# Two result chains in one-bank tiles, taken out block by block, and a half sum made from another sum

## The chip, the cores and the metric

The kernel runs on one core of a Trainium2 chip. The metric is the device time in microseconds (us) of one execution. TensorE (PE in the profile) multiplies, VectorE (DVE) adds and subtracts, ScalarE (ACT) applies functions and casts, GpSimd (POOL) issues the gathers and scatters, and SyncE (SP) issues most of the loads. Each engine takes its instructions strictly in the order in which they are written in this kernel, and waits in place where an operand is not ready.

## The reference

For 4096 tokens of 1024 features, after a layer norm:

```python
q, k, v = xn @ Wq.T + bq, xn @ Wk.T + bk, xn @ Wv.T + bv
kv_sum  = cumsum((elu(k) + 1) * v, axis=1)
s = ((elu(q) + 1) * kv_sum * 64**-0.5) @ Wo.T + bo
h = gelu(buf @ w1.T + b1) @ w2.T + b2        # buf: tokens chosen by a router
g = silu(scattered(h, router weights))
out = x + s * g
```

The router keeps at most 256 tokens for each of 8 experts, so the products with `w1`, `w2`, `Wq` and `Wo` are needed for at most 2048 tokens: `g` is zero for the rest, and their `out` is `x`.

## The kernel before

**Stages.** A first stage (to 444.66 us) makes the norm, the keys, the values and their running sum, and the router's lists. The second, which the change is about, takes the 2048 chosen tokens in two passes (`p` = 0, 1) of 1024. A pass makes the feed-forward part in four slices (`hidden`, then `ffn_out`), then the queries (`queries`) and the output projection (`result`). Each of these ten steps of a pass is a 1024x1024x1024 product, done as seven half-size products by a scheme of Strassen's kind: a weight or token quarter, or a sum of quarters (`t`, and sums written into the quarters' own places), against another. So there are 2 x 10 x 7 = 140 half-size products. The text numbers them 1 to 140 in order of time: 57 to 63 are the queries of pass 0 and 64 to 70 its output projection; 127 to 133 and 134 to 140 are the same of pass 1. "The crossing" is the stretch from the queries to the output projection, around products 62 to 66 and again around 132 to 136.

**A product.** It is 48 matmuls of 128x128 on 128x512 (L1023). Each float is split into a high part (a cast on ACT, L799) and the rest (a subtraction on DVE, L802, called "low" here), and three of the four part products are made, hence 2 halves `u` x 4 blocks `m` x 2 x 3 = 48. Half `u` of an operand is cast and split while the product before runs: `cast0`, `low0`, `cast1`, `low1` in the list below. The usual order is all four blocks of half 0, then all four of half 1; only the very last product goes block by block.

**Results.** A product's result is a tile `ps` of four PSUM banks, one for each block of 512. Products that are added up without anything in between form a chain in one tile (`chains`); PSUM has room for two such tiles (pool `fps`), and the built program uses them by turns: every product writes the four banks that the one before did not write. DVE takes a result out in one instruction (L951: `plus`, or `more` and `last` in `features`).

**The order of the work** is written out by hand. `multiply(n)` issues product n; then the hooks of step n follow, phase by phase: `load`, `pre`, `cast0`, `evac`, `low0`, `add`, `cast1`, `low1`, `post`, `raw`. `on(n, phase, f)` puts a piece of work there. So what stands in phase `evac` of step n takes out product n-1 while product n runs, and on ACT and DVE everything waits for what stands earlier.

**Around the crossing.** `features` takes the last results of the queries out with `last`: product 61 at step 62, 62 at step 63, and 63 at step 64. For each, `act` of `queries` runs a Relu and an Exp for each of four blocks on ACT (L1257, L1258), and `then` at phase `post` of the same step makes four DVE operations L1263 and two L1268. The quarter `(0, 1)` comes from product 63. `left_tokens` then makes three half sums on DVE from the four finished quarters: `t` = h01 + h11 (L951) at `post` of step 64, behind `then`, and h01 = h00 - h01 and h00 = t - h00 (L948 twice) at `pre` of step 65. h00, so changed (S2 here), is the left operand of product 66, and h01, so changed (S3), that of product 68. `result` takes product 64 out twice at step 65 (`e1`: three DVE instructions, the last of which writes `y`), product 65 at step 66 (`c11`), and so on; `done` scatters a quarter to DRAM with four indirect DMAs from POOL that add to what lies there (L1328), after the whole quarter is ready.

**The end.** `last` in `result` takes products 138 and 139 out in one piece each, and the last product, 140, in four blocks.

**The start.** The second stage's two PSUM tiles lie where the first stage had its pools `trp` (banks 0 to 3) and `mmp` (banks 4 to 7). The first stage's last value products are in `mmp`, and DVE takes them out in L401.

## Time and profile before

Three runs gave 2052.49, 2051.97 and 2054.68 us, a median of 2052.49. The execution with a profile took 2053.1 us, of which 2051.3 us are the span from its first to its last instruction.

| engine | busy us | share of the span |
|---|---|---|
| PE | 1968.8 | 96% |
| DVE | 1513.0 | 74% |
| ACT | 756.7 | 37% |
| POOL | 398.3 | 19% |

The profile's timeline lists instructions as "start, duration, engine, line, operation, what it writes and reads, count", with the idle time of the engine before it, and what ended that, in square brackets; equal neighbours are merged. The view by stretches of time gives, for each stretch, each engine's busy time and number of instructions, the share of full speed at which TensorE's clock was granted (PEclk), and the DMA engines' busy share and rate. A product that waits for nothing takes 10.88 us (48 matmuls, 0.227 us from start to start).

### The profile page before, as it was taken

To read this page: it belongs to the slowest core of one execution; us is meant where nothing else is said; L and a number is where in the kernel's file an instruction comes from. 1 tells how busy PE (TensorE), PEld (TensorE's weight loads), DVE (VectorE), ACT (ScalarE), POOL (GpSimd) and SP (SyncE) were. 2 spreads that over 40 slices of the span, in tenths; PEclk is the share of its full clock that TensorE was granted. 3 is DMA by queue.
4 is the path that set the end of the run, shared out by engine and by line. 5 is a ranking of instruction groups with operands and counts; after the bars stand their busy time and mean duration, and the time that the engine had idled before them with its cause. 6 is when DMAs were issued, how large, how long until landed. Compare 5 with 4: busy or idle time off the path is not lost.

```text
span 2051.3 us, 22262 instructions
## 1 busy us (share of the span) xinstructions
PE 1968.8 (96%) x8840; PEld 1624.9 (79%) x8840; DVE 1513.0 (74%) x1378; ACT 756.7 (37%) x874; POOL 398.3 (19%) x359
## 2 busy tenths in 40 slices
PE   7999999999999999999999799999999999999875
PEld 6877878888887887888888578888888888888664
DVE  7868876679867867875877786775774775786784
ACT  2323332225433524433433453342432432433451
POOL 1001104654002402713040027300000003040013
PEclk9999999999999999999999989999999999999988
DMA  8867848657249349347156049427326327336314
GB/s 308 241 195 239 268 124 189 194 153 299 80 166 362 108 164 343 121 153 282 46 184 254 23 110 307 168 75 249 127 87 249 116 100 257 116 124 235 124 21 63
DMA packets 113842, 360.31 MB, mean 176 GB/s; under 512 B 12768, under 2 KB 37344, under 8 KB 95584
## 3 DMA queue, kind: packets, MB, share of 16 engines
q1 hardware_dynamic: 77504, 299.98, 42.2%
q0 software_dynamic: 17792, 42.55, 7.8%
q10 hardware_dynamic: 18432, 16.26, 3.5%
q8 instruction: 72, 1.18, 0.2%
q14 instruction: 42, 0.34, 0.1%
HBM read 292.66 MB, written 73.42 MB: 178 GB/s over the span
## 4 chain that ended last, share of the span: by engine, by line
PE 78%; DVE 11%; ACT 3%; DMA 3%; issue 3%; POOL 0%; ACTq 0%; SPq 0%; DVEq 0%; POOLq 0%
PE ps L1023 62%; PE pk L160 3%; PE pk L161 3%; PE pk L162 3%; PE pv L162 2%; PE pv L160 2%; PE pv L161 2%; DMA b<-xtd 1%; DVE hid L951 1%; DVE a L802 1%; DVE hid L1263 1%; DVE b L802 1%; DVE raw L948 1%; DMA xtd<-b 1%; PE pl L326 1%
## 5 line engine op out<-in xcount | busy, mean ns | idle before, releaser
L1023 PE MATMUL ps<-b,a 128*128 128x512 f32 x6720 | 1541.1, 392 | 44.2 <-DVE y L951 20.7
L1023 PEld LDWEIGHTS ps<-b,a 128*128 128x128 f32 x6720 | 1269.0, 189 | 315.9 <-ACT b L799 21.5
L799 ACT CAST a<-raw 128x1024 fp32r<-128x1024 f32 x140 | 147.2, 1052 | 434.6 <-PE ps L1023 376.1
L802 DVE TENSOR_TENSOR a<-raw,a 128x1024 fp32r<-128x1024 f32 x140 | 170.6, 1221 | 171.2 <-ACT a L799 171.2
L648 POOL DMA_INDIRECT gk<-kvs,eighth x128 | 156.4, 1222 | 657.8 <-DVE kv L240 620.0
L799 ACT CAST a<-hid 128x1024 fp32r<-128x1024 f32 x120 | 126.0, 1050 | 358.0 <-PE ps L1023 250.4
L802 DVE TENSOR_TENSOR a<-hid,a 128x1024 fp32r<-128x1024 f32 x120 | 146.5, 1221 | 63.8 <-ACT a L799 63.6
L802 DVE TENSOR_TENSOR b<-raw,b 128x1024 fp32r<-128x1024 f32 x140 | 170.7, 1220 | 1.9 <-ACT b L799 1.9
L951 DVE TENSOR_TENSOR hid<-ps,hid 128x2048 f32<-128x2048 f32 x54 | 123.5, 2286 | 54.4 <-PE ps L1023 54.4
L948 DVE TENSOR_TENSOR raw<-raw,raw 128x2048 f32<-128x2048 f32 x70 | 160.3, 2289 | 1.0
L799 ACT CAST b<-raw 128x1024 fp32r<-128x1024 f32 x140 | 146.6, 1047 | 2.1 <-DMA xtd<-b 2.1
L951 DVE TENSOR_TENSOR work<-ps,work 128x2048 f32<-128x2048 f32 x40 | 91.5, 2288 | 48.8 <-PE ps L1023 48.8
L160 PE MATMUL pk<-xt,ws_w 128*128 128x512 f32 (+1 forms) x264 | 102.4, 388 | 1.5 <-ACT xt L166 1.5
L161 PE MATMUL pk<-xt,ws_w 128*128 128x512 f32 (+1 forms) x264 | 102.0, 386 | 1.3 <-DVE xt L167 1.3
L162 PE MATMUL pv<-xt,ws_w 128*128 128x512 f32 (+1 forms) x264 | 101.4, 384 | 1.3 <-DVE ws_w L167 1.2
L162 PE MATMUL pk<-xt,ws_w 128*128 128x512 f32 (+1 forms) x264 | 101.8, 386 | 0.0
L160 PE MATMUL pv<-xt,ws_w 128*128 128x512 f32 (+1 forms) x264 | 101.6, 385 | 0.0
L161 PE MATMUL pv<-xt,ws_w 128*128 128x512 f32 (+1 forms) x264 | 101.2, 383 | 0.0
L166 ACT CAST ws_w<-wr_w 128x1024 fp32r<-128x1024 f32 x64 | 66.1, 1049 | 70.0 <-issue 30.8
L167 DVE TENSOR_TENSOR ws_w<-wr_w,ws_w 128x1024 fp32r<-128x1024 f32 x64 | 77.8, 1215 | 14.7 <-ACT ws_w L166 14.7
L680 POOL DMA_DIRECT2D xtd<-o x28 | 24.2, 888 | 283.3 <-DVE o L167 276.3
L362 ACT ACTIVATE kb<-pk,bs 128x512 f32<-128x512 f32 (+1 forms) x40 | 25.8, 645 | 140.8 <-PE pk L162 106.5
(185 smaller groups left out, 1656.4 us busy)
## 6 DMA issues: line engine op xcount, KB each, us to landing
b<-xtd SPq DMA_DIRECT2D x126, 1024.0 KB, 5.5
raw<-in_w SPq DMA_DIRECT2D x64, 1024.0 KB, 5.2
wr_w<-in_wk SPq DMA_DIRECT2D x32, 512.0 KB, 4.6
wr_w<-in_wv SPq DMA_DIRECT2D x32, 512.0 KB, 4.6
xtd<-b SPq DMA_DIRECT2D x14, 1024.0 KB, 7.7
xtd<-o POOLq DMA_DIRECT2D x28, 512.0 KB, 9.1
kvs<-kr ACTq DMA_DIRECT2D x32, 256.0 KB, 4.9
raw<-in_wq SPq DMA_DIRECT2D x8, 1024.0 KB, 5.1
```

Of the source, the lines that this page charges most:

```text
L160: nc.tensor.matmul(ps, ws[:, 0, k], mv[:, 0, k, c0:c1], start=k == 0, stop=False)
L161: nc.tensor.matmul(ps, ws[:, 0, k], mv[:, 1, k, c0:c1], start=False, stop=False)
L162: nc.tensor.matmul(ps, ws[:, 1, k], mv[:, 0, k, c0:c1], start=False, stop=k == DC - 1)
L166: nc.scalar.copy(dst[0], src)
L167: nc.vector.tensor_tensor(dst[1], src, dst[0].bitcast(F32), ALU.subtract)
L362: nc.scalar.activation(kb, ps, AF.Identity, bias=bcol)
L648: nc.gpsimd.indirect_dma_start(out=dst, out_offset=None, in_=src, in_offset=bass.IndirectOffsetOnAxis(ap=idx, axis=0),)
L799: nc.scalar.copy(self.parts[0], src)
L802: nc.vector.tensor_tensor(self.parts[1], self.src, self.parts[0].bitcast(F32), ALU.subtract)
L948: nc.vector.tensor_tensor(dst, a, b, ALU.subtract)
L951: nc.vector.tensor_tensor(dst, a, b, ALU.add)
L1023: nc.tensor.matmul(ps[:, m], a(h, k, m), b(l, k), start=s["first"] and u == 0 and k == 0 and i == 0, stop=u == 1 and k == 1 and i == 2, sk ...
```

## The change

Three things are changed.

1. Each of the two places of four banks gets a pool of its own. `banks` gives a new chain the place that the preceding product does not write, either as one tile of four banks or, where the chain is marked `apart`, as four tiles of one bank. Marked are the chain of products 61 and 63 (and 131 and 133), and the chain of products 136, 138 and 140.
2. Marked chains are taken out a block at a time. In the queries, product 61 goes out in four instructions in place of one, and product 63 is multiplied block by block and taken out, each block with its own Relu and Exp, at four spots: `add`, `low1` and `post` of step 63 and `pre` of step 64. At the end, products 136, 138 and 139 are taken out by blocks, and blocks of 138 and 139 are scattered one by one.
3. In all ten output steps, S2 is made first, at `pre` of the old step, and S3 one step later, as h11 - S2, which is the same as h00 - h01.

In the built program the first product's place is banks 4 to 7, and products alternate from there; before, it was banks 0 to 3. No other engine than PE, DVE and ACT has another order.

```diff
-    fps = ctx.enter_context(tc.tile_pool(name="fps", bufs=2, space=PSUM, reuse_waits="tile"))
+    places = [[None, None, ctx.enter_context(ExitStack())] for _ in range(2)]
+    last_place = [0]
+    def banks(apart):
+        i = last_place[0] = 1 - last_place[0]
+        place = places[i]
+        if place[0] != apart:
+            place[2].close()
+            place[:2] = apart, place[2].enter_context(
+                tc.tile_pool(
+                    name=name("fps"), bufs=1, space=PSUM, side=("left", "right")[i],
+                    reuse_waits="tile",
+                )
+            )
+        if apart:
+            return i, [
+                place[1].tile([P, BT], F32, tag=f"ps{m}", name=name("ps")) for m in range(4)
+            ]
+        return i, place[1].tile([P, 4, BT], F32, tag="ps", name=name("ps"))
...
-            s["ps"][0] = fps.tile([P, 4, BT], F32, tag="ps", bufs=2, name=name("ps"))
+            s["place"][0], s["ps"][0] = banks(s["apart"])
+        last_place[0] = s["place"][0]
...
-        if n == len(plan):
+        if s["apart"] and s["last"]:
             order_of.sort(key=lambda um: um[1])
...
-        on(n0 + 2, "pre", lambda: sub(h[0, 1], h[0, 0], h[0, 1]))
         on(n0 + 2, "pre", lambda: sub(h[0, 0], h["t"], h[0, 0]))
+        on(n0 + 3, "pre", lambda: sub(h[0, 1], h[1, 1], h[0, 0]))
...
-            plus(h[key], ps[k][0], h[base])
+            for m, x in blocks(ps[k][0]):
+                plus(h[key][:, m], x, h[base][:, m])
...
-        on(n0 + 8, "evac", lambda: last(7, (0, 1), (0, 1)))
+        if not then:
+            on(n0 + 8, "evac", lambda: last(7, (0, 1), (0, 1)))
+            return h
+        def block(m):
+            key = (0, 1)
+            plus(h[key][:, m], ps[7][0][m], h[key][:, m])
+            act(h[key], h[key], *key, blocks=(m,))
+        for d, phase, m in ((7, "add", 0), (7, "low1", 1), (7, "post", 2), (8, "pre", 3)):
+            on(n0 + d, phase, lambda m=m: block(m))
...
-            rows_of = range(4) if n0 + k == len(plan) else [slice(0, 4)]
-            for v in rows_of:
-                plus(c[base][:, v], ps[k][0][:, v], c[base][:, v])
+            parts = blocks(ps[k][0])
+            if p == NP - 1 and k == 6:
+                parts = [(m, ps[k][0][:, m]) for m in range(4)]
+            for v, x in parts:
+                plus(c[base][:, v], x, c[base][:, v])
                 nc.vector.tensor_tensor(c[base][:, v], c[base][:, v], y[key][:, v], ALU.mult)
-            done(key, lambda m: c[base][:, m])
+                done(key, lambda m: c[base][:, m], range(4) if len(parts) == 1 else (v,))
```

More of the change, by code (lines that the diff above doesn't have):

```diff
@@ L911, in tile_first_tokens, with blocks @@
     )
-    fps = ctx.enter_context(tc.tile_pool(name="fps", bufs=2, space=PSUM, reuse_waits="tile"))
+    places = [[None, None, ctx.enter_context(ExitStack())] for _ in range(2)]
[16 more added lines that the diff above has]
+        return i, place[1].tile([P, 4, BT], F32, tag="ps", name=name("ps"))
+    def blocks(ps):
+        if isinstance(ps, list):
+            return [(m, x) for m, x in enumerate(ps)]
+        return [(slice(0, 4), ps)]
     bq1, nbq = (cp.tile([P, DC], F32, name=n) for n in ("bq1", "nbq"))
@@ L1023, in multiply @@
                     nc.tensor.matmul(
-                        ps[:, m],
+                        ps[m] if s["apart"] else ps[:, m],
                         a(h, k, m),
@@ L1037, in tile_first_tokens, with chains @@
     COLS = (1, 2, 6, 5, 7, 3, 4)
-    def chains(n0, order, groups):
-        where = {i: [None] for g in groups for i in g[:1]}
+    def chains(n0, order, groups, apart=False):
         for g in groups:
+            where, place = [None], [None]
             for i in g:
                 k = order.index(i)
-                plan_at(n0 + 1 + k).update(first=i == g[0], ps=where[g[0]])
+                plan_at(n0 + 1 + k).update(
+                    first=i == g[0], last=i == g[-1], ps=where, place=place,
+                    apart=apart and order[-1] in g,
+                )
     def left_weights(n0, src, order):
@@ L1133, in features @@
         if order == ROWS:
-            chains(n0, order, ((1, 2), (6, 7, 4), (5, 3)))
+            chains(n0, order, ((1, 2), (6, 7, 4), (5, 3)), then is not None)
         else:
@@ L1186, in hidden, with outputs @@
         )
-    def outputs(n0, h, src, ahead=0):
+    def outputs(n0, h, src, ahead=0, final=False):
         left_tokens(n0, h)
         right_weights(n0, src, ahead)
-        chains(n0, COLS, ((1,), (2,), (6, 7, 4), (5, 3)))
+        chains(n0, COLS, ((1,), (2,), (6, 7, 4), (5, 3)), final)
         return {k: plan_at(n0 + k)["ps"] for k in range(1, 8)}
@@ L1245, in turn, with act @@
                     )
-        def act(dst, src, i, j):
-            if dst is src:
-                r = [small("ex") for _ in range(2)]
-                r = [r[m // 2][:, m % 2 * BT : (m % 2 + 1) * BT] for m in range(4)]
-            else:
-                r = [dst[:, m] for m in range(4)]
-            kvt["r", i, j] = r
-            for m in range(4):
+        def act(dst, src, i, j, blocks=range(4)):
+            if 0 in blocks:
+                if dst is src:
+                    r = [small("ex") for _ in range(2)]
+                    r = [r[m // 2][:, m % 2 * BT : (m % 2 + 1) * BT] for m in range(4)]
+                else:
+                    r = [dst[:, m] for m in range(4)]
+                kvt["r", i, j] = r
+            r = kvt["r", i, j]
+            for m in blocks:
                 e = 4 * i + m
@@ L1300, in result @@
     def result(n0, h, y, p):
-        ps = outputs(n0, h, wo[0], 1)
+        ps = outputs(n0, h, wo[0], 1, final=p == NP - 1)
         c = {}
@@ L1320, in e1, with done @@
             plus(c[0], ps[1][0], over_blocks(c["b"][:, :BT]))
-        def done(key, parts):
+        def done(key, parts, rows_of=range(4)):
             i, j = key
-            for m in range(4):
+            for m in rows_of:
                 src = parts(m)
@@ L1350, in more @@
             c[key] = h["t" if key == (0, 1) else (0, 1)]
+            if isinstance(ps[k][0], list):
+                for m, x in blocks(ps[k][0]):
+                    plus(c[key][:, m], x, c[1][m // 2][:, m % 2])
+                return
             for half in range(2):
```

## The prediction, made before the changed kernel ran

> **What bounds the kernel now.** I read the page first: PE is busy for 96% of the span, and the chain of work that ended last lies on it but for two kinds of places.

> ```profile
> PE 78%; DVE 11%; ACT 3%; DMA 3%; issue 3%; POOL 0%; ACTq 0%; SPq 0%; DVEq 0%; POOLq 0%
> ```

> The 11% of DVE are in the crossings. PE's own timeline shows it for pass 0: products 62 and 63 run through, and from there every start waits, up to 10.48 us ahead of product 66.

> ```profile
> 1118.50 22.25 PE L1023 MATMUL ps<-b,a 128*128 128x512 f32 x97 [0.96 <-DMA b<-xtd]
> 1141.67 5.74 PE L1023 MATMUL ps<-b,a 128*128 128x512 f32 x24 [0.93 <-DVE b L802]
> 1147.99 5.51 PE L1023 MATMUL ps<-b,a 128*128 128x512 f32 x23 [0.57 <-DVE b L802]
> 1157.53 0.76 PE L1023 MATMUL ps<-b,a 128*128 128x512 f32 x1 [4.03 <-DVE hid L951]
> 1159.71 12.41 PE L1023 MATMUL ps<-b,a 128*128 128x512 f32 x47 [1.41 <-DVE b L802]
> 1182.59 0.76 PE L1023 MATMUL ps<-b,a 128*128 128x512 f32 x1 [10.48 <-DVE y L951]
> 1184.77 720.72 PE L1023 MATMUL ps<-b,a 128*128 128x512 f32 x3167 [1.41 <-DVE b L802]
> ```

> From the start of 62 (1118.50) to that of 67 (1198.07) are 79.57 us for five products of 10.88, so 25.2 us are lost; in pass 1 (1906.61 to 1986.26) 25.3. Some of it is clock. The view by stretches, here product 33, which follows a wait of 2.54 us, and product 66:

> ```profile
> 800.11:812.73 12.62, 12.62 (x49) 10.22 (x49) 9.17 (x11) 4.91 (x7) 2.54 (x3) 0.86 1.02 408
> ```

> ```profile
> 1182.59:1198.07 15.48, 14.07 (x48) 11.01 (x49) 13.66 (x12) 12.80 (x19) 7.22 (x4) 0.76 0.37 50
> ```

> PEclk is the number after POOL's: granted 0.86 and 0.76. Product 33 took 1.74 us too long without a wait inside.

> DVE's timeline then says what the 10.48 us wait for: takings-out of 61, 62 and 63, and `t`, S3 and S2 one behind the other.

> ```profile
> 1122.36 2.28 DVE L951 TENSOR_TENSOR hid<-ps,hid 128x2048 f32<-128x2048 f32 x1
> ...
> 1137.07 2.28 DVE L951 TENSOR_TENSOR hid<-ps,hid 128x2048 f32<-128x2048 f32 x1
> ...
> 1155.10 2.28 DVE L951 TENSOR_TENSOR hid<-ps,hid 128x2048 f32<-128x2048 f32 x1
> ...
> 1171.04 2.29 DVE L951 TENSOR_TENSOR ht<-hid 128x2048 f32<-128x2048 f32 x1
> 1173.37 2.29 DVE L948 TENSOR_TENSOR hid<-hid 128x2048 f32<-128x2048 f32 x1
> 1175.69 2.29 DVE L948 TENSOR_TENSOR hid<-ht,hid 128x2048 f32<-128x2048 f32 x1
> ```

> Between these DVE waits for ACT (3.95 us twice, 5.10 once): the eight Relu and Exp of a quarter (5.13 us in a row) stand ahead of the casts.

> **The change, part by part.**

> *Places.* Products took the two places by turns before and do so after; only the sides are swapped. By itself this is worth nothing: pools are re-opened for products 61, 65, 131, 135 and 136, which in the built order wait for the same results as before. The exception is the start. Product 1 began at 444.66 without a wait, in banks 0 to 3. It now goes to banks 4 to 7, which DVE empties last in:

> ```profile
> 447.11 0.44 DVE L401 SCALAR_TENSOR_TENSOR kb<-pv,bs,kb 128x256 f32<-128x256 f32 x1
> ```

> It ends at 447.55; PE follows DVE by about 0.15 (63 is out at 1155.10 + 2.28 = 1157.38, and 65 starts at 1157.53), so product 1 starts at 447.7: **+3.0 us**. Nothing hides it: the casts, loads and takings-out of the second stage are timed by its products, and shift along. Does the clock drop after it? [...] 2.54 us before product 33 cost 1.74, while 0.96 before 62 cost 0.1 (10.98 us). I take the row: **+1.7**; ends 0 and 3.4 [...]. Start: +4.7, from 3.0 to 6.4.

> *S2 ahead of S3 in the ten output steps.* In the ordinary ones PE does not wait, and S3 is needed two products later. Its 2.3 us of DVE come back ahead of a taking-out that is then due at the old time. One gain: product 10 waited 0.45 us (with its tail 0.6) for ACT, whose copy of a result stood behind the cast of S2; that goes: **-0.6**. In the crossings it is in the sum below.

> *The crossing, pass 0* (before -> after), adding durations in each queue's order:
> - Taking 61 out: starts at 1122.36 as before, but block 0 is done after 0.69 instead of 2.28, so ACT's Relu and Exp start 1.6 earlier, the cast behind them too, and the low that DVE waits for: 1130.88 -> 1129.3. Taking 62 out: 1137.07 -> 1135.5. (Four blocks cost DVE 0.24 more, start to start, hidden by this wait.)
> - Product 63, block by block, needs its second half 1.4 us after its start (1129.48) instead of 5.4: cast by 1129.3, low by 1130.5, in time. Its load is issued at 1124.23 as its place comes free; with the median 5.5 us it lands at 1129.7, needed at 1130.8. With the 7 us of product 62's it stalls 0.5, which the next wait swallows: taken as 0.
> - Low for 64: done at 1140.0, so its wait goes. Blocks 0 and 1 of 63 go out at 1139.9 and 1140.5. But block 0's Relu and Exp (1.29) stand on ACT ahead of 64's second casts: that low 1146.71 -> 1146.4. `then` of 62 ends at 1152.6; block 2, the 2.2 us difference L948, block 3: block 3 done at 1156.1, where 63 as a whole was done at 1157.4.
> - ACT: block 3's Relu and Exp, then both casts for 65: to 1159.4 (these casts stood ahead of the Exp before). So 65's second matmul: 1159.71 -> 1160.9, **later**. DVE goes on without the old wait of 3.95: `then` of 63 starts 1165.88 -> 1163.0; `t` 1171.04 -> 1168.2; S2 1175.69 -> 1170.5, as S3 is gone. `e1`, `y` and the lows follow at once: `y` done 1177.3, 66's second matmul 1184.77 -> 1179.6: -5.2.
> - PE idles about 3.5 us instead of 10.5 ahead of 66, and is at half speed for an estimated 3.7 us after it instead of 5.4: 2.65 lost -> 1.85. Product 67: 1198.07 -> 1192.1. S3 is now in front of 67's lows, done at 1191.2, still ahead of 1192.1.
> So **-6.0**; ends -4.5 [...] and -7. Pass 1 has the same rows 788 us later: **-6.0**. Reading a bank while PE writes its neighbour is shown nowhere before; the nearest row is the end's block, 0.69 us, which I take; a fifth more would be 0.1 a block.

> *The end.* Before, POOL issues eight DMAs from here to there, 1.86 us each:

> ```profile
> 2023.99 1.56 POOL L1328 DMA_INDIRECT out<-ht,half  x1 [2.60 <-DVE ht L1359]
> ...
> 2038.19 1.56 POOL L1328 DMA_INDIRECT out<-y,half  x1 [0.30 <-issue]
> ```

> Now 138's four go from 2008.1 (before 2013.68), done by 2015.4. 139 is out at 2019.1; its block 0 is added and multiplied by 2020.5, so its first DMA is at 2020.8: 3.2 earlier. Product 140's blocks 0 and 1 are ready when POOL is, 2 and 3 at 2028.7 and 2031.4; eight times 1.86 put the last issue at 2033.9, 4.3 earlier. But the DMA engines are 0.94 to 1.04 busy from 2030 to 2042, about 2.1 us a DMA, and the last of their packets ends at 2043.8, 17.9 after the first of these eight: so the end moves with the first: **-3.6**; ends -2 and -4.5. Costs of the extra DVE instructions: DVE waited 1.8 and 6.3 there.

> *Sum*: +4.7 - 0.6 - 12.0 - 3.6 = -11.5. The span 2051.3 becomes 2039.8 and the profiled execution's 2053.1 becomes 2041.6; the median lies 0.6 below that: **2041.0**.

> **The rivals.** (1) As above, 0.6: 2041. (2) The crossing gives half, 0.22: with the Exp of blocks 0 and 3 put ahead of casts, ACT becomes what DVE waits for, as 65's later start shows. That leaves 3 us each: 4.7 - 0.6 - 6 - 3.6 = -5.5, **2047**. Against it: in the walk DVE waits there for under 2 us. (3) No clock drop at the start, and shorter ones in the crossings, 0.13: 1.7 at the start, 2 x 0.85 in the crossings and 0.6 at the end make 4.0 more, **2037**. (4) Slower, 0.05: the clock. The idle ahead of 65 grows from 4.0 to 6.6 us; should TensorE then stay at half speed through 65 and 66, 65 ends at 1160.9 + 21.3 = 1182.2, 66 follows at once and ends at 1204, 6 us later than before: 4.7 - 0.6 + 12 - 3.6 = +12.5, **2065**. It decides once half speed outlasts 65; before, it lasted under 4 us after 65's second matmul.

> **Chances and range.** A measurement of this kernel tells 0.2% (4 us) from no change. (1), (3) and most of (2) are faster: 0.92; 0.03 the same, 0.05 slower. The better ends together (3.0 at the start, -7 twice, -4.5) give 2036.4, and (2) 2047; half a microsecond is added on each side, which leaves out (4) and the tails of (2) and (3).

> **What would show it.** Product 1 starting 3 us after the last value product; lows of 65 later and S2 5 us earlier against 62's start; the wait ahead of 66 at 3 to 5 us; 62 to 67 in 73.6 us; the first `ht` DMA 2 us after 139's end. Wrong if product 1 starts at once, if 62 to 67 takes over 77 us, or if the last bytes land no earlier after 140.

## The result and the profile after

Four runs of the changed kernel gave a median of 2040.62 us (2038.86 to 2042.59), four of the kernel before on the same chip 2053.59 (2051.97 to 2054.71): a ratio of **0.9938 [0.9921, 0.9955]**. The execution with a profile took 2040.5 us with a span of 2038.6, 12.7 less than before; the prediction's sum was -11.5.

The chain of work that ended last has 5 points more of PE and 3 fewer of DVE:

```profile
PE 83%; DVE 8%; ACT 3%; issue 2%; DMA 2%; POOL 1%; ACTq 0%; DVEq 0%; SPq 0%; POOLq 0%
```

PE's timeline, at the start and in both crossings:

```profile
447.50 196.08 PE L1051 MATMUL ps<-b,a 128*128 128x512 f32 x864 [2.68 <-DVE kb L401]
...
1119.93 28.03 PE L1051 MATMUL ps<-b,a 128*128 128x512 f32 x121 [1.17 <-ACT a L799]
1148.89 5.52 PE L1051 MATMUL ps<-b,a 128*128 128x512 f32 x23 [0.94 <-DVE b L802]
1160.63 0.79 PE L1051 MATMUL ps<-b,a 128*128 128x512 f32 x1 [6.22 <-ACT b L799]
1162.08 12.95 PE L1051 MATMUL ps<-b,a 128*128 128x512 f32 x47 [0.66 <-DVE b L802]
1178.61 0.47 PE L1051 MATMUL ps<-b,a 128*128 128x512 f32 x1 [3.58 <-DVE y L978]
1180.78 721.00 PE L1051 MATMUL ps<-b,a 128*128 128x512 f32 x3167 [1.70 <-DVE b L802]
...
1961.62 0.77 PE L1051 MATMUL ps<-b,a 128*128 128x512 f32 x1 [4.22 <-DVE y L978]
1963.80 26.50 PE L1051 MATMUL ps<-b,a 128*128 128x512 f32 x106 [1.41 <-DVE b L802]
```

Product 1 now waits for L401. The wait ahead of 66 is 3.58 us in place of 10.48, and that ahead of 65 is 6.22 in place of 4.03. 62 starts at 1119.93 and 67 at 1194.39: 74.46 us for 79.57 before; in pass 1, from 1902.76 to 1976.76, 74.00 for 79.65. The view by stretches, for product 66 from its first matmul to 67's, shows that the clock is still lost there (PEclk is 0.78; it was 0.76):

```profile
1178.61:1194.40 15.79, 14.09 (x49) 11.14 (x50) 15.58 (x13) 12.80 (x19) 5.54 (x4) 0.78 0.26 35
```

DVE's timeline of the crossing of pass 0 shows the takings-out in pieces, and where DVE itself still waits for ACT:

```profile
1123.58 2.48 DVE L978 TENSOR_TENSOR hid<-ps,hid 128x512 f32<-128x512 f32 x4
...
1141.16 1.28 DVE L978 TENSOR_TENSOR hid<-ps,hid 128x512 f32<-128x512 f32 x2
1146.48 1.23 DVE L802 TENSOR_TENSOR a<-hid,a 128x1024 fp32r<-128x1024 f32 x1 [4.04 <-ACT a L799]
...
1156.60 0.68 DVE L978 TENSOR_TENSOR hid<-ps,hid 128x512 f32<-128x512 f32 x1
1159.67 1.23 DVE L802 TENSOR_TENSOR a<-hid,a 128x1024 fp32r<-128x1024 f32 x1 [2.38 <-ACT a L799]
...
1169.38 2.29 DVE L978 TENSOR_TENSOR ht<-hid 128x2048 f32<-128x2048 f32 x1
1171.71 2.29 DVE L975 TENSOR_TENSOR hid<-ht,hid 128x2048 f32<-128x2048 f32 x1
...
1176.18 2.28 DVE L978 TENSOR_TENSOR y<-ps,bo 128x2048 f32<-128x2048 f32 x1
```

`t` and S2 follow one another without S3, and S2 is done at 1174.00. At the end, POOL's timeline has the first of the last eight DMAs at 2011.29, before 2023.99:

```profile
2011.29 1.56 POOL L1374 DMA_INDIRECT out<-ht,half  x1 [4.61 <-DVE ht L1411]
...
2025.50 1.56 POOL L1374 DMA_INDIRECT out<-y,half  x1 [0.30 <-issue]
```

From 137's start to the last packet of these DMAs it takes 54.01 us (1976.76 to 2030.77), before 57.56 (1986.26 to 2043.81).

| term, us of the span | predicted | measured |
|---|---|---|
| wait ahead of product 1 | +3.0 | +2.84 (444.66 to 447.50) |
| clock at product 1 | +1.7 | 0 (product 1 takes 10.96, before 10.91) |
| wait at product 10 | -0.6 | -0.54 (start of 1 to start of 18: 185.58 to 185.04) |
| crossing, pass 0 | -6.0 | -5.11 |
| crossing, pass 1 | -6.0 | -5.65 |
| the end, from 137 to the last packet | -3.6 | -3.54 |
| clock at product 19 | none | -1.28 (12.62 to 11.34) |
| the rest | 0 | +0.6 (0.34 of it behind the last packet) |
| sum | -11.5 | -12.7 |

### The profile page after: what moved, and what is told of

It is laid out like the page before. It is cut to its first block, busy times and chain, and to the rows that moved or that the text cites. A ratio compares the mean times of both kernels' runs of the same rounds, so it can differ in the third digit from the quotient of the medians.

```text
span 2038.6 us, 22297 instructions
## 1 busy us (share of the span) xinstructions
PE 1967.2 (96%) x8840; PEld 1623.9 (80%) x8840; DVE 1514.1 (74%) x1404; ACT 757.8 (37%) x874; POOL 396.7 (19%) x359
## 4 chain that ended last, share of the span: by engine, by line
PE 83%; DVE 8%; ACT 3%; issue 2%; DMA 2%; POOL 1%; ACTq 0%; DVEq 0%; SPq 0%; POOLq 0%
PE ps L1051 66%; PE pk L160 3%; PE pk L161 3%; PE pk L162 3%; PE pv L162 2%; PE pv L160 2%; PE pv L161 2%; DVE hid L1309 1%; PE pl L326 1%; DVE a L802 1%; DVE raw L975 1%; DVE hid L978 1%; DMA xtd<-o 1%; ACT ex L1303 1%; DMA b<-xtd 1%
## 5 line engine op out<-in xcount | busy, mean ns | idle before, releaser
L1051 PE MATMUL ps<-b,a 128*128 128x512 f32 x6720 | 1539.2, 391 | 36.4 <-ACT b L799 12.7
L802 DVE TENSOR_TENSOR a<-raw,a 128x1024 fp32r<-128x1024 f32 x140 | 170.6, 1221 | 169.6 <-ACT a L799 169.6
L802 DVE TENSOR_TENSOR a<-hid,a 128x1024 fp32r<-128x1024 f32 x120 | 146.4, 1220 | 61.8 <-ACT a L799 61.7
L802 DVE TENSOR_TENSOR b<-raw,b 128x1024 fp32r<-128x1024 f32 x140 | 170.5, 1218 | 1.8 <-ACT b L799 1.8
L978 DVE TENSOR_TENSOR hid<-ps,hid 128x2048 f32<-128x2048 f32 (+1 forms) x69 | 125.0, 1821 | 54.9 <-PE ps L1051 54.9
L166 ACT CAST ws_w<-wr_w 128x1024 fp32r<-128x1024 f32 x64 | 66.1, 1049 | 70.3 <-issue 30.9
L680 POOL DMA_DIRECT2D xtd<-o x28 | 24.2, 888 | 285.5 <-DVE o L167 278.7
```

Source lines behind the costliest of these rows:

```text
L166: nc.scalar.copy(dst[0], src)
L802: nc.vector.tensor_tensor(self.parts[1], self.src, self.parts[0].bitcast(F32), ALU.subtract)
L978: nc.vector.tensor_tensor(dst, a, b, ALU.add)
L1051: nc.tensor.matmul(ps[m] if s["apart"] else ps[:, m], a(h, k, m), b(l, k), start=s["first"] and u == 0 and k == 0 and i == 0, stop=u == 1 ...
```

## The experiments

Theory: the three parts act as the prediction has them, apart from each other; what is left in the crossing is ACT's queue ahead of 65 and the clock after the waits. Rivals: one part makes all of the gain; the order of ACT doesn't matter; what is lost after a wait isn't the clock.

The yardsticks are stretches of the trace. "62 to 67" is the time from the start of 62 to the start of 67, half speed included. "66's second matmul" is its start counted from 62's start, which is free of what the clock does behind it. In two profiles of the kernel before, it comes at 66.1 to 66.3 us in all four crossings; 62 to 67 takes 79.4 to 79.75, and 137 to the last packet 57.2 and 57.6.

The runs fall into four sets. In three of them (the parts; the whole again, the sides exchanged, the casts first and the first `fill`; the last run) every kernel, that before too, took some 30 us longer. In the traces of these sets the first stage ends 9 to 15 us later, and products 74 to 76 take 42 to 54 us in place of 32.6, where PE mostly waits for nothing that the profile shows ("issue") and then runs at half speed. It is not the changed order: the changed kernel itself takes 32.64 us for them in its first trace and 45.05 in its second. What makes it stays open. Whole times of one kernel spread by 9 to 26 us in these sets, so the stretches say more.

**One part alone.** The places alone, which is the changed kernel with the old takings-out and half sums:

```diff
-        if s["apart"] and s["last"]:
+        if n == len(plan) or s["apart"] and s["last"]:
...
+        on(n0 + 2, "pre", lambda: sub(h[0, 1], h[0, 0], h[0, 1]))
         on(n0 + 2, "pre", lambda: sub(h[0, 0], h["t"], h[0, 0]))
-
-        on(n0 + 3, "pre", lambda: sub(h[0, 1], h[1, 1], h[0, 0]))
...
-            chains(n0, order, ((1, 2), (6, 7, 4), (5, 3)), then is not None)
+            chains(n0, order, ((1, 2), (6, 7, 4), (5, 3)))
...
-        if not then:
+        if True:
...
-        ps = outputs(n0, h, wo[0], 1, final=p == NP - 1)
+        ps = outputs(n0, h, wo[0], 1, final=False)
...
-            if p == NP - 1 and k == 6:
+            if p == NP - 1 and k == 7:
```

> Part 1 of the change alone: a pool for each place and the rule for the place, every chain in one tile of four banks, results taken out whole, S3 before S2 as before. Theory (the crossing is a chain of DVE and ACT work, the places alternate anyway): nothing but the new wait of product 1, so 2.8 us slower than before; product 1 starts 2.8 us later, products 62 to 67 take 79.6 us as before, the last bytes come 25.5 us after the last product's start as before. Rival (the gain comes from the places): 62 to 67 takes about 74 us, and the time is about 8 us below before.

S2 ahead of S3 alone, in the kernel before:

```diff
-        on(n0 + 2, "pre", lambda: sub(h[0, 1], h[0, 0], h[0, 1]))
         on(n0 + 2, "pre", lambda: sub(h[0, 0], h["t"], h[0, 0]))
+
+        on(n0 + 3, "pre", lambda: sub(h[0, 1], h[1, 1], h[0, 0]))
```

> Part 3 alone: S2 first and S3 from it a step later, all else as before. Theory: product 10's wait goes (0.5 us), and in each crossing DVE reaches y and the lows of 66 2.3 us earlier; 66's second matmul comes 2.3 us earlier, with the clock 2 to 3 us are gained, so 62 to 67 takes 76.6 to 77.6 us, and in all 4.5 to 6.5 us are gained. Rival (all of the crossing's gain comes from the blocks, S3 being hidden behind other waits): only 0.5 us gained.

The query blocks with the places, which is the changed kernel without S2 first and without the blocks at the end: the edit of the places alone, but without its third and fourth piece (`chains` and `if True`).

> The places and the blocks of products 61 and 63 (131 and 133); S3 before S2, and the end, as before. Theory: the wait at the start costs 2.8 us; in each crossing DVE starts t 2.8 us earlier and 66's second matmul comes 2.8 us earlier, so 62 to 67 takes 76 to 77.5 us; in all 2 to 4 us gained. Rival (blocks are what matters): 62 to 67 takes 74 us as with the whole change, 8 us gained. Rival (blocks only move the wait, since 65 starts later): 62 to 67 takes 79 us or more, 2 us lost.

The blocks at the end with the places, without the query blocks and without S2 first: the edit of the places alone, but without its first piece and its last two.

> The places and the blocks at the end (products 136, 138, 139, 140); queries and S3 as before. Theory: 2.8 us lost at the start, 3.5 us gained at the end: from the start of product 137 to the last packet 54.0 us in place of 57.6; in all 0.7 us gained, which can't be told from no change by the times. Rival (the DMA engines set the end): the last packet comes 57 us after 137's start, 2.5 us lost in all.

And the whole again, in the second of the sets:

> The changed kernel again, as the base for the runs beside it. Theory: it stays ahead of the kernel before by some 12 us of 2052 (ratio 0.994, taken over its stretches): product 1 waits 2.7 us, 62 to 67 takes 73.6 to 75, 137 to the last packet 54.0, whatever the rest of the execution does. If the clock decides by where its windows of 3.41 us fall, product 1 takes 10.9 or 12.6 us; a rule by the length of the wait alone would give the same each time.

| kernel | ratio to before, 95% | wait ahead of 1 | product 1 | 66's second matmul | 62 to 67, pass 0 and 1 | 137 to last packet |
|---|---|---|---|---|---|---|
| places alone | 1.0007 [0.9992, 1.0022] | 2.69 | 12.58 | 66.24, 66.23 | 79.10, 78.50 | 57.47 |
| S2 first alone | 0.9972 [0.9954, 0.9989] | none | 10.9 | 63.87, 63.81 | 76.84, 77.07 | 57.03 |
| query blocks | 0.9993 [0.9974, 1.0012] | 2.68 | 11.0 | 63.33, 63.19 | 75.91, 76.76 | 56.99 |
| end blocks | 0.9994 [0.9978, 1.0011] | 2.70 | 12.61 | 66.14, 66.15 | 78.24, 79.42 | 53.94 |
| whole, again | 0.9959 [0.9943, 0.9975] | 2.67 | 11.0 | 60.94, 60.98 | 73.35, 73.95 | 53.82 |

The parts add up: against 66.2, S2 first gives 2.4 us a crossing, the query blocks 2.9 to 3.0, and both together 5.2 to 5.3. Only the end blocks shorten the end, by 3.1 to 3.6. The places cost their 2.7 us at the start in every kernel of the table that has them, so that neither the query blocks nor the end blocks alone can be told from no change in the whole time. The rival of one part that makes all of the gain falls. The places alone leave 66's second matmul where it was, while 62 to 67 takes 0.5 to 1.1 less: that is the clock behind it, where half speed lasts 4.5 and 3.2 us in place of 5.4 and 5.9.

**The wait at the start.** The changed kernel with the two sides exchanged, so that product 1 writes banks 0 to 3:

```diff
-                    name=name("fps"), bufs=1, space=PSUM, side=("left", "right")[i],
+                    name=name("fps"), bufs=1, space=PSUM, side=("right", "left")[i],
```

> The changed kernel with the sides of the two places exchanged, so that product 1 writes banks 0 to 3. Theory: the wait ahead of product 1 is only a question of which banks it writes; it goes, product 1 starts some 0.1 us after the last value product, and the rest is as in the changed kernel (62 to 67 in 73.6 to 75, 137 to the last packet 54.0): 2.8 us less than the changed kernel, 4.5 where the clock had dropped at product 1. Rival: the four banks that DVE empties last are only needed one product later, and product 2 waits instead: then nothing is gained.

Ratio 0.9934 [0.9910, 0.9959]; median 2070.7, the whole beside it 2074.3. Product 1 starts at 456.54, 0.12 after the start of the last value matmul, and 1 to 18 takes 184.99: product 2 doesn't wait. The wait is only the choice of banks; the rival falls. This is read from the trace: the ratio's interval overlaps that of the whole beside it (0.9943 to 0.9975).

**The order on ACT.** The run with the sides exchanged, and in it blocks 0 and 3 of product 63 behind the casts (their takings-out on DVE move with them):

```diff
-        for d, phase, m in ((7, "add", 0), (7, "low1", 1), (7, "post", 2), (8, "pre", 3)):
+        for d, phase, m in ((7, "low1", 0), (7, "low1", 1), (7, "post", 2), (8, "evac", 3)):
```

> As the run with the sides exchanged, and in the crossings block 0 of 63 goes out after the low of 64's second half, and block 3 at the place of the taking-out of step 64, behind the casts of 65, so that no Relu and Exp stands ahead of a cast that PE waits for. Theory (the later second matmul of 65 is these Relu and Exp on ACT): 65's second matmul comes at 38 to 39 us after 62's start instead of 42.2, 66's at 57.5 to 58 instead of 60.9, 62 to 67 takes 71 us: 6 us less for the two crossings, 9 less than the changed kernel. Rival (DVE's own queue is what 66 waits for, ACT is idle enough): 65 comes earlier but 66's second matmul stays at 60.5 to 61, and PE only waits longer ahead of 66.

Ratio 0.9912 [0.9885, 0.9939]; median 2063.2, 11.1 below the whole beside it, whose interval it does not touch. PE's timeline in pass 0:

```profile
1128.82 27.69 PE L1051 MATMUL ps<-b,a 128*128 128x512 f32 x121 [0.98 <-DMA b<-xtd]
...
1165.67 0.79 PE L1051 MATMUL ps<-b,a 128*128 128x512 f32 x1 [3.40 <-ACT b L799]
1167.43 13.31 PE L1051 MATMUL ps<-b,a 128*128 128x512 f32 x47 [0.97 <-DVE b L802]
1184.54 0.76 PE L1051 MATMUL ps<-b,a 128*128 128x512 f32 x1 [3.79 <-DVE y L978]
1186.71 28.60 PE L1051 MATMUL ps<-b,a 128*128 128x512 f32 x119 [1.41 <-DVE b L802]
```

65's second matmul comes at 38.6 after 62's start (42.3 and 42.4 with the sides exchanged alone), 66's at 57.9 (61.0), in both passes; 62 to 67 takes 70.0 and 70.2 (73.3 and 74.4). DVE's waits for the casts fall with it: ahead of the lows of 64's second half from 4.04 us in the changed kernel to 2.78, and ahead of 65's from 2.38 to 0.50. Those 3.1 us are what 66 gains, so the casts that PE and DVE waited for stood behind Relu and Exp: shown. The change left 3 us a crossing there.

**Product 61 by blocks.** The changed kernel with the Relu and Exp of 61 in reverse order of blocks (in `act` of `queries`), so that ACT starts after the last of the four:

```diff
-            for m in blocks:
+            for m in reversed(blocks) if (i, j) == (1, 1) else blocks:
```

> The changed kernel with the four Relu and Exp behind product 61 (and 131) in the order of blocks 3, 2, 1, 0: ACT then starts 1.8 us later, after the last of the four takings-out, as it did before the change. Theory (the takings-out of 61 by blocks is what lets ACT's casts, and with them the lows of 63's second half, come in time for a product that goes block by block): the second half of 63 is 1 to 1.6 us late, 63 itself stalls by that, and all that follows is later: 66's second matmul at 61.9 to 62.5 us after 62's start, 62 to 67 in 74.5 to 76. Rival (that start is swallowed by DVE's later waits): 63 stalls under 0.3 and 66's second matmul stays at 60.9.

Ratio 0.9970 [0.9959, 0.9981]. 63 is stalled by 1.0 and 1.2 us, as expected; 66's second matmul comes at 62.8 and 62.9, 1.9 later, somewhat above the expected 61.9 to 62.5; 62 to 67 takes 75.6 and 76.0. So the earlier start of ACT behind 61 carries through to 66; nothing swallows it. It makes 1.9 of the 2.9 to 3.0 us of the query blocks, which leaves some 1.0 for the blocks of 63.

**The clock after a wait.** In the changed kernel, matmuls of a zero weight (`room`, a tile set to zero earlier) are added to product 65's sum while PE waits for 66:

```diff
+    def fill(n, count=22):
+        s = plan_at(n)
+        b = s["bview"](s["b"][1].t)
+        for j in range(count):
+            nc.tensor.matmul(
+                s["ps"][0][:, 3], room[:, :P], b(0, 1),
+                start=False, stop=j == count - 1, skip_group_check=True,
+            )
...
     def multiply(n):
         s = plan_at(n)
+        if n in (66, 136):
+            fill(n - 1)
```

> The changed kernel with 22 matmuls of a zero weight (5.0 us) added to the sum of product 65 (and 135), in the time in which PE waits ahead of 66 (and 136); the results are unchanged. Theory (the loss after the wait is the clock[...]): no half speed after 66's second matmul; it stays at 60.9 us after 62's start, and 67 follows 10.7 us later instead of 13.6 and 12.9: 62 to 67 in 71.5 us, 5 us less for the two crossings. Rival (what is lost after 66 is not the clock, or what is left of the wait is enough to drop it): 67 stays at 74 to 74.5 after 62, and where the added matmuls are themselves late, 66's second matmul is later by up to 1 us.

Ratio 0.9928 [0.9902, 0.9954], which overlaps the whole's beside it; the trace tells them apart. PE's timeline, with the added matmuls in the third line:

```profile
1171.30 0.79 PE L1062 MATMUL ps<-b,a 128*128 128x512 f32 x1 [6.23 <-ACT b L799]
1172.75 12.89 PE L1062 MATMUL ps<-b,a 128*128 128x512 f32 x47 [0.66 <-DVE b L802]
1185.48 5.15 PE L1041 MATMUL ps<-b,room 128*128 128x512 f32 x22
1190.46 0.39 PE L1062 MATMUL ps<-b,a 128*128 128x512 f32 x1
1191.44 11.18 PE L1062 MATMUL ps<-b,a 128*128 128x512 f32 x48 [0.59 <-DVE b L802]
1203.11 22.05 PE L1062 MATMUL ps<-b,a 128*128 128x512 f32 x96 [0.49 <-DVE b L802]
```

66's second matmul stays at 61.0, and 62 to 67 takes 71.8 in both passes (73.35 and 73.95 in the whole beside it), with no half speed behind 66. It was the clock. But the last line has a new wait of 0.49, and product 67 takes 11.66: DVE's lows for 67 stand behind S3, and they are what is late once 66 is faster. Of 1.6 and 2.1 us won a crossing, 0.8 are given back.

**All of these together.** The run with the casts first, with `fill` as above, 24 added matmuls ahead of 66 and 136 and 8 ahead of 19 and 33, and S3 at the end of its step:

```diff
+    FILL = {19: 8, 33: 8, 66: 24, 136: 24}
...
+        if n in FILL:
+            fill(n - 1, FILL[n])
...
-        on(n0 + 3, "pre", lambda: sub(h[0, 1], h[1, 1], h[0, 0]))
+        on(n0 + 3, "post", lambda: sub(h[0, 1], h[1, 1], h[0, 0]))
```

> The run with the casts first, and the added zero matmuls ahead of 66 and 136 (24 each) and ahead of 19 and 33 (8 each, 1.8 of the 2.5 us that PE waits there for a load), and S3 at the end of step 66 in place of its start; the results are unchanged. In the run with matmuls added ahead of 66, product 67 then waited for its lows, which stand behind S3 on DVE (11.66 us in place of 10.88), so that 0.8 us of the gain were given back. Theory: 66's second matmul at 57.9 us after 62's start, 62 to 67 in 68.6 us (70.0 and 70.2 without the added matmuls), 67 in 10.9; 33 in 10.9 in place of 12.6 and 19 in 10.9: 4.7 to 6.4 us less than with the casts first alone. Rival: another thing on DVE is next behind S3, 67 stays at 11.5 or more, and S3 moved back makes 68 or another step's fifth product late: then under 3 us.

Beside it, the kernel before once more:

> The kernel before again, for its trace beside those of these runs. Theory: the stretches are those of the first profile (62 to 67 in 79.6 us or up to 1 less where the clock's windows fall well, 66's second matmul at 66.2, 137 to the last packet 57.5, no wait ahead of product 1); what makes these executions some 30 us longer lies elsewhere, around products 74 to 76 and ahead of product 1, as in the other kernels' traces. Rival: it lies in the changed kernels' own order, and this trace has no stall around 75.

In this set the kernel before took 2052.1, and its second trace is like the first, without a stall around 75; nor has any other trace of the set one. The record names chip 3 for this set and for that of the parts, so the longer times do not go with the chip's number. The kernel with everything took 2025.6: ratio **0.9870 [0.9855, 0.9885]**, the lowest of all. Its trace is of an execution of 2031.8, the slowest of its four. There its crossing takes 68.65 in pass 0, as worked out, and 67 no longer waits, with S3 out of its way. In pass 1 it takes 70.3: 132 waits 2.24 for a load (0.98 in the changed kernel), runs at half speed, and shifts what follows so that the added matmuls end 0.7 early. So of the 4.7 to 6.4 us expected over the casts first, this trace shows the 1.4 of pass 0. 33 gained nothing and 18 to 21 took 46.9, since 20 and 34 then waited 0.61 and 1.35 for their loads. One reason for these waits was of the fill's own making: it held the operand in whose place the load goes. So, with the other operand:

```diff
-        ps, b = s["ps"][0], s["bview"](s["b"][1].t)
+        ps, b = s["ps"][0], s["a"][1].t[:, 1, :BT]
-                ps[3] if s["apart"] else ps[:, 3], room[:, :P], b(0, 1),
+                ps[3] if s["apart"] else ps[:, 3], room[:, :P], b,
```

> The run with all four places filled, with one thing changed: the added zero matmuls read a left operand of the product before in place of its right one. With the right one, the place that the load for product 20 (and 34) goes to came free only after the added matmuls, and that load was issued 0.4 us ahead of 19's start in place of 2.2; so 20 and 34 waited 0.6 and 1.35 us for it, and nothing was gained there. Theory (that wait is of the fill's own making, and the half speed of 19 and 33 is a real loss): the load is issued 2.2 us ahead again, 20 and 34 wait under 0.3, 18 and 19 take 24.2 us together in place of 25.1, 33 11.0 in place of 12.5; 62 to 67 in 68.6 in both passes: 2.4 us less than with the right operand, some 28 less than the kernel before. Rival (the loads set the pace there, and half speed only filled the time until they land): 20 and 34 wait as long as 19 and 33 are faster, 18 and 19 stay at 25 or more, and only the crossings' gain is left.

Ratio 0.9878 [0.9856, 0.9900], no better. 62 to 67 takes 68.6 in pass 0 and 67.4 in pass 1. The load is issued 2.1 and 2.6 us ahead again, and yet, in PE's timeline around 33:

```profile
810.81 1.98 PE L1043 MATMUL ps<-a,room 128*128 128x512 f32 x8
813.58 11.12 PE L1064 MATMUL ps<-b,a 128*128 128x512 f32 x48 [0.80 <-DMA b<-xtd]
826.07 24.31 PE L1064 MATMUL ps<-b,a 128*128 128x512 f32 x106 [1.37 <-DMA b<-xtd]
```

33 runs at full speed (11.12), and 34 waits the 1.37 that were saved: products 32 to 35 take 48.0 us, in the two traces of the kernel before 48.0 and 47.8. There the rival holds: the loads set the pace, and half speed only fills the time. At 18 to 21 it is 46.4, as in the changed kernel (46.3), where the clock had not dropped; before, with the drop, 47.5 and 47.6. The 2.2 us ahead of 132 are there again (0.98 with the casts first alone); whether S3's new place or the added matmuls make them was not told apart.

## Why the prediction was right, point by point

- **Start.** The +3.0 were right: 2.84, and 2.67 to 2.70 in the part kernels. The **+1.7 of clock failed**, as the prediction's own end for it (0, an estimate like the other, 3.4) allowed. The prediction took the row of product 33 as if a wait's length decided. Six kernels have nearly the same wait ahead of product 1: it took 12.6 in three (places alone, end blocks, and the fill, whose wait was 3.1) and 11.0 in the other three. What differs is where the wait lies against the windows of 3.413 us, as two of the traces show. These are the two windows around the start with the places alone, then three of the changed kernel (PE's busy time comes first, PEclk behind POOL's):

```profile
455.39:458.81 3.42, 0.73 (x5) 0.53 (x4) 3.31 (x6) 0.00 (x0) 0.00 (x0) 1.00 1.00 412
458.81:462.22 3.41, 3.41 (x9) 2.63 (x8) 0.80 (x3) 0.00 (x0) 2.28 (x4) 0.50 0.94 173
```

```profile
442.70:446.11 3.41, 2.13 (x18) 1.92 (x17) 3.37 (x4) 0.00 (x0) 1.55 (x2) 1.00 1.03 423
446.11:449.52 3.41, 2.02 (x9) 1.73 (x10) 2.41 (x7) 0.00 (x0) 0.60 (x1) 1.00 0.94 277
449.52:452.93 3.41, 3.41 (x17) 2.83 (x16) 0.69 (x1) 1.78 (x2) 2.33 (x5) 1.00 0.99 226
```

With the places alone one window holds the whole wait of 2.69 (79% idle), and half speed follows; in the changed kernel a boundary at 446.11 cuts the wait into 1.3 and 1.4 (at most 41% idle), and nothing follows. Half speed also followed the window ahead of product 19 in the kernel before (640.60 to 644.02), which was idle for 61%.
- **S2 first.** Right in both places: product 10 no longer waits, and alone it moves 66's second matmul by 2.4, the 2.3 of one difference.
- **The crossing's queues.** Right to 0.3 us in each step that was looked at. Against 62's start, which moved by 1.43, 65's second matmul was due at 1162.3 and came at 1162.08; 66's was due at 1181.0 and came at 1180.78. The later 65, +0.9 to +1.3 us against 62, was foreseen. For PE it was harmless, since 65 had ended 3.6 us before 66 could start; the order on ACT that made it late also held DVE back, and with it 66, as the run with the casts first shows.
- **The crossing's clock.** This term was mis-sized: half speed after 66's second matmul was to last 3.7 us and cost 1.85, a length for which the prediction gives no working. It lasted 6.0 us (to 1186.8) and cost 2.97 in pass 0, and 4.65 and 2.31 in pass 1, where the kernel before lost 2.65 and 2.90; so the crossings gave 5.1 and 5.7, not 6.0 (the end of 4.5 was an estimate). The wait is shorter by two thirds, but half speed followed it just the same: behind the window from 1176.56 to 1179.97, idle for 86%, until the end of the one from 1183.39 to 1186.80, which had no idle time; in pass 1 behind 1958.22 to 1961.63, idle for all but 0.01 us, until the end of 1965.04 to 1968.45, again without idle time. The fill shows that this loss is the clock: with it, the 48 matmuls from 66's second on took 11.18 us.
- **The end.** Right in size: -3.54 for -3.6. The end moves with the first of the last eight DMAs, 3.2 earlier against 139, as predicted; the other 0.4 of the 3.6 has no working, and the 17.9 us from the first of the eight to the last packet are 19.8 from its issue. That the DMA engines are what holds back the rest is not shown. POOL's eight issues were to put the last one 4.3 us earlier (seven steps of 1.86); they took 14.2 us in both kernels, so it came 3.2 earlier too, and the last packet ended 5.3 us behind it (before 5.6).
- **The sum.** The predicted time was 1.2 us too high. Larger errors stand behind that, and they cancel: 1.7 of clock at the start that did not come and 1.28 won at product 19 made the kernel faster than predicted; 1.2 less in the crossings and 0.6 in the rest made it slower. At product 19 the same wait (2.08, then 2.06) lay over two windows after the change (idle for 15% and 46%) and within one before (61%). That is luck and no part of the change, and so is a sum so near to the measurement.
- **Rivals.** (2), ACT as what DVE waits for, was put off with "under 2 us"; after the change DVE waits 2.38 ahead of 65's lows and 4.04 ahead of 64's. It did not halve the gain, since that was in the walk, but the mechanism is real: 3 us a crossing were still to be had. (3) was half right: no drop at the start, but the drops in the crossings did not get shorter. (4), the clock slower than before, did not decide: after 65's second matmul half speed lasted 4.2 us, and 66 still waited 3.6 for `y`.

## What to carry to other kernels

Walk each queue instruction by instruction from the trace, and do it against a fixed event: the queues came out to 0.3 us, while the larger errors were all in the clock. Ahead of a matmul that waits, put casts before functions on ACT, and ask what is late next when a wait goes: behind 66 it was S3, behind 33 a load. In these traces a wait that left PE idle for 61% or more of a window of 3.413 us cost again behind it (1.7 us where PE waited 2.1 to 2.7 once, 2.97 behind the waits of 3.58 and 1.70 at 66), but only where nothing else set the pace: at 33 a load did, and products 32 to 35 took 48.0 us at full speed too.

## What the runs showed of the hardware

- Waits of 2.1 to 2.7 us ahead of a product halved the clock or did not, by their place: windows of 3.413 us that were idle for 61% (product 19, before), 73% (33, before) and 79% (1, places alone) were followed by half speed, those idle for 46% (19, changed kernel) and 41% (1, changed kernel) were not.
- Counted in the traces of the kernel before and of the changed kernel, over the windows from 435 us to the last drop, with PE's idle time as the profile has it: of the windows at full speed, the 13 that were idle for 61% or more were all followed by half speed, and none of the other 897, idle for 49% or less, was.
- Of the windows at half speed in these two traces from 435 us on, but for those behind the last drop, which comes after PE's last matmul, each of the 11 that were idle for 16% or less ended it, and behind each of the 12 that were idle for 24% or more half speed went on for another 3.4 us at least, as behind 1179.97 to 1183.39 in the changed kernel (76% busy).
- Reading a bank while PE writes another of the same set of four cost nothing that the trace shows: block 0 of 63 was taken out in 0.68 us at 1141.16, while block 3 was multiplied until 1141.96; the row of before, with PE at rest, has 0.69.
